# A four-layer image network: the mixers' statistics taken from their Fourier modes, and where the third layer's tiles lie

## The chip, the cores and the metric

One Trainium2 chip, one of its cores, one kernel launch. The time is the device time of one execution in microseconds (us), the median of three runs. The engines are PE (matrix products and transposes, results in PSUM), ACT (one activation function per pass, with a scale and a bias per partition), DVE (vector work, reductions and normalisation statistics), POOL (slower vector work), and SP, which here only starts transfers. A transfer can be started from SP's queue or from ACT's; the start itself then stands in that engine's queue. All data is 32-bit float.

## The reference

Four images of 64 x 64 positions with 128 channels go through four residual layers, `x = x + layer_n(_gn(x))`, where `_gn` is a group normalisation over groups of four channels: a selective-scan layer, a Fourier layer with a feed-forward part, an attention between channels in Fourier space ("CoDANO"), and a neighbourhood attention. The change is in the third one. There every channel is a token, a 64 x 64 picture, and every `instance_norm` is over a picture. What matters is its end, after the attention:

```python
def instance_norm(x, g, b):
    mu = jnp.mean(x, axis=(-2, -1), keepdims=True)
    var = jnp.var(x, axis=(-2, -1), keepdims=True)
    return (x - mu) * jax.lax.rsqrt(var + EPS) * g[:, None, None] + b[:, None, None]

def spectral_conv(x, w, out_shape):
    wc = w[..., 0] + 1j * w[..., 1]          # 32 x 17 modes
    ...
    xft = jnp.fft.rfftn(x, axes=(-2, -1), norm='forward')
    top = jnp.einsum('bihw,iohw->bohw', xft[:, :, :mh, :mw], wc[:, :, :mh])
    bot = jnp.einsum('bihw,iohw->bohw', xft[:, :, -mh:, :mw], wc[:, :, mh:])
    ...
    return jnp.fft.irfftn(out_ft, s=out_shape, axes=(-2, -1), norm='forward')

def fno_layer(x, spec_w, skip_w, skip_b, out_shape, norm=None, act=None):
    xs = fourier_resample(conv1x1(x, skip_w, skip_b), out_shape)
    xf = spectral_conv(x, spec_w, out_shape)
    if norm is not None:
        xf = instance_norm(xf, *norm)
    y = xf + xs
    return act(y) if act is not None else y

# inside codano_forward, at its end
attn = instance_norm(attn + tokens, attn_norm_g, attn_norm_b)
m = instance_norm(attn, norm2_g, norm2_b)
m = fno_layer(m, mixer_w1, mixer_skip_w1, mixer_skip_b1, (H, W), norm=(mixer_norm_g1, mixer_norm_b1), act=_gelu)
m = fno_layer(m, mixer_w2, mixer_skip_w2, mixer_skip_b2, (H, W), norm=(mixer_norm_g2, mixer_norm_b2))
out = instance_norm(m, mixer_out_g, mixer_out_b) + attn
```

The mean and the variance of `xf` are functions of its few modes: by Parseval, the mean is the mode (0, 0), and the variance is a weighted sum of the squares of the others.

## The kernel before

The code counts its layers from 0 and this text from one: the first layer is `layer0`, the second `layer1`, the third `layer2`, the fourth `layer3`. In the profile the first layer takes the span up to 5752 us, the second 5752 to 6230, the third 6230 to 7211, the fourth the rest.

**Memory and waits.** Tiles come from pools, laid one after another in a partition's bytes. A pool opened where a closed pool lay must wait for the old users of those bytes. With `reuse_waits="tile"` each tile waits only for the users of the earlier tiles under it; otherwise all tiles of the new pool wait for all users of the pools it falls on. The second layer's pools wait by tile; the third's (`layer2`, L1713) and the fourth's (L1735) by pool. In the second layer the pool `l1big` comes first, then `l1tmp`.

**Second layer** (`layer1`, L962). For each image `layer1_spectrum` makes `hT` (two buffers in `l1tmp`) from the image `x1`, the weights `w1` and `w2` and, for its second axis, a transposed copy `xa` of the image. `layer1_feed` then goes through eight chunks c of 512 positions: four products into `pf`, four Relu on ACT (L914) into `h1`, sixteen products into `po` (L926), a layer norm on DVE, the addition to x (L945), and a store on SP's queue (L946). The feed of one image runs beside the spectrum of the next; the last image's feed has nothing beside it. SP's queue is in the order written; the other engines are put in order by a scheduler. `layer2_weights` (L1005) loads and prepares the third layer's constants meanwhile.

**Third layer** (`layer2`, L1713). `layer2_image` (L1202) is a generator that yields between steps, and two images run in turn. `Pace` (L1112) holds a model of each engine's costs; its `in_turn` always advances the image whose modelled time is earliest, and that fixes the order in which PE, ACT, DVE and POOL run their work. A `yield True` says that the next step needs the last one's result; `nc.aside` marks work that does not move the image's modelled time. All its instructions are recorded at one line, L1155, so groups are told apart by tile names.

The mixers begin after the attention's `z` has its statistics. `spectral` (L1607) takes a picture tile (`z`, later `m`; 128 positions x 32 x 128 channels):

- `dft_y`: eight groups of four products into `pu`, each copied by ACT into `U`.
- four `pq` (two products of 512 columns each), each multiplied by the mode weights on DVE into `Zp` (68 rows: real and imaginary parts in four forms times 17 frequencies; 64 channel pairs x 32).
- `synthesis`: four steps, each two `pa` (copied by ACT into `S`, tile tag S2) and two `pb`, one for u = 0 and one for u = 1; a `pb` holds four position blocks of 128 channels and goes to the function `put`. For `spectral` that is `copied`: ACT copies it into `sp`, DVE counts it with four bn_stats, and a piece of side work is given to POOL.

`token_stats` turns the counts into mean and variance with eight small products `in_pm` and two DVE operations between them; `norm_scale` takes the square root on ACT and the reciprocal on DVE.

Mixer 1 scales `sp` with q1 and f1 and adds it to `m` (= z times A2) chunk by chunk (four chunks of 1024): even chunks by eight ACT activations (`affine`), odd ones by two whole-chunk DVE operations (`by_rows`), then an addition on DVE and the gelu on ACT. Its side work is `residual` (L1642): it loads the layer's input `xr` and makes `z*sa + za + xr` on POOL. Mixer 2's side work is `grown`, `m * scal(10)` on POOL. Mixer 2 adds `sp*q2` to `m` by 32 scalar_tensor_tensor (stt) on DVE, counts `m` with 32 bn_stats, and the end makes `m*q3 + f3 + z`: three chunks by ACT and a DVE addition, the last by eight stt and one `by_rows` on DVE; each chunk is stored from SP.

The fourth layer's constants and edges are loaded at its start (L1760 and following).

Of the kernel before, what the change touches and what calls it, by code (L numbers as in the profile page):

```python
# [11 lines left out]
F32 = mybir.dt.float32  # L12
# [5 lines left out]
P = 128  # L18
# [782 lines left out]
def layer1_weights(sh, A, wp, wq):  # L801
# [4 lines left out]
    for name, pool in (("w1", wp), ("w2", wq)):  # L806
        w[name] = pool.tile([P, 16, 2, P], F32, name=name)
        nc.sync.dma_start(w[name], A[name])
# [8 lines left out]
    w["sy"] = wq.tile([P, 256], F32, name="c_sy1")  # L817
# [4 lines left out]
def layer1_spectrum(sh, w, pools, x_dram, x, norm, out):  # L822
# [17 lines left out]
    hT = out["hT"] = tmp.tile([P, NT], F32, name="hT", bufs=2)  # L840
    for axis in range(2):
# [18 lines left out]
        if axis == 0:  # L860
            out["xa"] = big.tile([P, NJ, DM], F32, name="xa", bufs=1)
            xv = x_dram.rearrange("(h w2 w1) d -> w1 h w2 d", w1=2, w2=32)
            for q in range(2):
                nc.sync.dma_start(out["xa"][64 * q : 64 * q + 64], xv[q])
# [40 lines left out]
def layer1_feed(sh, w, pools, x, hT, x_out):  # L905
# [12 lines left out]
    for c in range(NCH):  # L918
# [27 lines left out]
        nc.sync.dma_start(x_out[c * CH : (c + 1) * CH, :].rearrange("(j p) d -> p j d", p=P), xc)  # L946
# [14 lines left out]
def layer1(sh, A, x_in, x_out, l2w, wt, ahead):  # L961

    tc, nc = sh.tc, sh.nc
    with ExitStack() as ctx:
# [4 lines left out]
        pools |= {"small": pool("l1small", 2), "ps": pool("l1ps", 4, space=PSUM)}  # L969
        w = layer1_weights(sh, A, pools["tmp"], pools["big"])  # L970
# [3 lines left out]
        with tc.manual_schedule(engines=engines):  # L974
            for b in range(NB + 1):
                out = {}
# [13 lines left out]
                if b < NB:  # L990
                    fed = layer1_feed(sh, w, pools, x, out["hT"], x_out(b))
# [13 lines left out]
def layer2_weights(sh, A, wp, setup, ps, wt, w):  # L1005
# [18 lines left out]
    for n in (1, 2):  # L1024
        load(f"mix{n}", [Q, 32], A[f"mix{n}"])
    pa, pb, vra, vrb, via, vib = (load(name, [Q, 32, 16], A[name], setup) for name in ("pa", "pb", "vra", "vrb", "via", "vib"))
# [22 lines left out]
    for n in (1, 2):  # L1049
        m = w[f"mix{n}"]  # L1050
        nc.vector.tensor_scalar(m, m, qc[:, 0:1], None, ALU.mult)
# [138 lines left out]
def layer2_image(sh, w, pools, x_in, x_out, scr, wt, parity, beside):  # L1190
# [75 lines left out]
    def dft_y(src, scale=None, then=None):  # L1266

        U = large("U2", [P, 2, 32, 64])
        for g in range(NJ // 4):
# [7 lines left out]
            else:  # L1277
                nc.scalar.activation(Ug, pg, AF.Copy, scale=scale)
                then(g)
# [327 lines left out]
    def spectral(src, mix, beside=()):  # L1607
        beside = iter(beside)
        U = yield from dft_y(src)
        Zm = own([Q, 64, 32], "Zp", tmp)  # L1610
        for g in range(4):
            px = ps.tile([Q, 32, 16], F32, name="pq", tag="b")
            for q in range(2):
                nc.tensor.matmul(
                    px, lhsT=w["quad"][:, q, :], rhs=U[:, q, :, 16 * g : 16 * g + 16], start=(q == 0), stop=(q == 1)
                )
            tt(
                Zm[:, 16 * g : 16 * g + 16, :],
                px.rearrange("p r t -> p t r"),
                mix.unsqueeze(1).to_broadcast([Q, 16, 32]),  # L1620
                ALU.mult,
            )
            yield g == 3
        sp = large("sp")
        st = own([P, NJ, 6], "in_st")

        def copied(u, g0, p):
            nc.scalar.copy(at(sp, u, g0), p)
            counted(st, sp, block(u, g0))
            nc.aside = True  # L1630
            next(beside, None)
            nc.aside = False

        yield from synthesis(Zm, copied)
        return sp, st


    m = large("m")
    for c in range(4):
        by_rows(m, z, A2, c, ALU.mult)  # L1640
    yield False
    def residual():  # L1642
        xr = large("xr")
        load_image(nc, xr, x_in)
        for n, c in enumerate(C4):
# [3 lines left out]
            if n % 2:  # L1649
                yield  # L1650

    sp, st = yield from spectral(z, w["mix1"], residual())
    mu, var = yield from token_stats(sp, st)
# [44 lines left out]
    yield True  # L1698
    for n, c in enumerate(C4):
        rows = slice(1024 * n, 1024 * n + 1024)  # L1700
        if n == 3:
# [7 lines left out]
        nc.sync.dma_start(x_out[rows, :].rearrange("(j p) d -> p j d", p=P), m[:, c, :])  # L1709
# [292 lines left out]
def constants():  # L2002
# [48 lines left out]
    qc[:, :, 6] = np.array([0, 1, 0, 1])[:, None]  # L2051
    c["c_qcol"] = qc.reshape(Q, 8)

# [14 lines left out]
def lay_out(i):  # L2068
# [52 lines left out]
    for n in (1, 2):  # L2121
        m = L2[f"mixer_w{n}"][0, 0].transpose(1, 0, 2)
        a[f"mix{n}"] = quad([m[..., 0], m[..., 1], m[..., 0], m[..., 1]])
    p = L2["proj_w"][:, 0].transpose(2, 1, 0, 3)
# [58 lines left out]
```

## Time and profile before

The profiled execution took 7781.59 us, of which the span is 7779.7; the three runs took 7775.43 to 7779.66 with a median of 7777.08. A table of the last three layers, from the windows of the trace and its start times:

| stretch | from | to | us |
|---|---|---|---|
| second layer | 5752 | 6230 | 478 |
| third layer, first pair: to its mixers' stretch | 6230 | 6475 | 245 |
| third layer, first pair: that stretch | 6475 | 6723 | 248 |
| third layer, second pair: to its mixers' stretch | 6723 | 6961 | 238 |
| third layer, second pair: that stretch | 6961 | 7211 | 250 |
| fourth layer | 7211 | 7780 | 569 |

A row of the window view gives the length of the window, each engine's busy time with the number of instructions, the clock that PE was granted as a share of full speed, and the transfer engines' load. A row of the timeline gives start, length, engine, line, operation, `out<-in` by the program's names, shapes, the number of instructions run together, and in brackets how long the engine had stood idle and what ended that. The chain of waits goes back from the last instruction to what released it; its rows are start, length and what it was. Where two durations overlap in a row, the records are those of a pipeline and the next start tells the pitch.

### The profile page before, as it was taken

The numbers are of one execution on the slowest core, as the hardware profiler recorded it, in microseconds if no ns is written. First come the engines' busy times: TensorE is split into PE (matmuls) and PEld (weight loads), VectorE is DVE, ScalarE is ACT, GpSimd is POOL, SyncE is SP. The second block draws the span as 40 slices with busy tenths as digits, with TensorE's granted clock in tenths as the row PEclk, the third lists the DMA queues.
The fourth block names the chain that finished last, engine by engine and source line by source line (L and its number), as shares of the span: only waits on it lengthen the run. The fifth ranks groups of instructions, "written<-read, shape, count | busy, mean of one in ns | idle before, by whom it ended". The sixth has DMA issues, their size and how long they took to land. (4 is left out here: it accounts for less than half of the span.)

```text
span 7779.7 us, 141035 instructions
## 1 busy us (share of the span) xinstructions
PE 6337.0 (81%) x52796; PEld 3998.2 (51%) x52796; DVE 6747.1 (87%) x8097; ACT 6112.9 (79%) x9715; POOL 5675.9 (73%) x2590
## 2 busy tenths in 40 slices
PE   7888888878889877888887777787779968687789
PEld 3544444444455444445554444444457756564566
DVE  7999999999999999999999999999966646556678
ACT  7999999989999998999999999999843323314667
POOL 4989999988999998999999999999930023223233
PEclk8999999999999999999999999999999978788899
DMA  6555556545565554555655445455532142231332
GB/s 171 173 163 175 174 173 176 170 169 165 186 183 179 185 177 162 163 177 179 180 184 180 168 156 185 160 188 177 181 107 63 43 128 61 71 108 40 103 95 81
DMA packets 1325855, 1158.87 MB, mean 149 GB/s; under 512 B 694133, under 2 KB 1119697, under 8 KB 1258226
## 3 DMA queue, kind: packets, MB, share of 16 engines
q1 hardware_dynamic: 1323010, 1148.47, 48.0%
q8 instruction: 416, 6.82, 0.4%
q14 instruction: 269, 2.20, 0.1%
q10 hardware_dynamic: 2160, 1.38, 0.1%
HBM read 956.37 MB, written 189.21 MB: 147 GB/s over the span
## 5 line engine op out<-in xcount | busy, mean ns | idle before, releaser
L688 DVE TENSOR_TENSOR_SCAN h<-dA,state,dB 128x512 f32<-128x512 f32 x4096 | 4921.0, 1266 | 204.4 <-POOL dB L682 79.5
L682 POOL TENSOR_TENSOR dB<-du,Bb 128x1024 f32<-128x1024 f32 x2048 | 4811.7, 2385 | 342.9 <-DVE h L688 208.6
L538 PE MATMUL pt<-ident,h 128*128 128x128 f32 x16384 | 2221.0, 279 | 875.7 <-ACT hT L548 860.0
L687 ACT ACTIVATE dA<-delta,A_neg 128x512 f32<-128x512 f32 x4096 | 2761.1, 697 | 157.6 <-DVE h L688 129.7
L538 PEld LDWEIGHTS pt<-ident,h 128*128 128x128 f32 x16384 | 1807.0, 142 | 1926.3 <-ACT hT L548 1704.7
L548 ACT COPY hT<-pt 128x1024 f32<-128x1024 f32 x2048 | 2080.2, 1016 | 164.7 <-PE pt L538 146.4
L573 PE MATMUL yT<-hT,W 128*32 128x256 f32 x16384 | 1379.6, 409 | 0.4
L573 PEld LDWEIGHTS yT<-hT,W 128*32 128x32 f32 x16384 | 456.0, 150 | 342.5 <-issue 330.9
L161 PE MATMUL cv<-xn,taps 128*128 128x512 f32 x936 | 527.0, 644 | 2.8 <-DVE delta L474 2.8
L1155 POOL TENSOR_TENSOR xg<-xg,so 128x1024 f32<-128x1024 f32 x16 | 39.3, 2466 | 636.5 <-PE pu L1155 613.6
L1900 POOL TENSOR_TENSOR S<-S,sm 128x784 f32<-128x784 f32 x128 | 191.1, 1493 | 419.1 <-DVE sm L1898 256.3
L477 POOL TENSOR_TENSOR du<-delta,u 128x1024 f32<-128x1024 f32 x128 | 304.3, 2377 | 79.0 <-DVE delta L474 78.9
L465 PE MATMUL dp<-xd,w_dt 65*128 65x512 f32 x512 | 288.8, 646 | 69.9 <-ACT Ct L456 47.0
L448 PE MATMUL xd_ps<-u,w_x 128*48 128x512 f32 x512 | 251.8, 615 | 23.6 <-DVE e L360 18.1
L1907 ACT ACTIVATE S<-S,mx 128x196 f32<-128x196 f32 x512 | 227.8, 448 | 35.9 <-DVE mx L1934 35.4
L161 PEld LDWEIGHTS cv<-xn,taps 128*128 128x128 f32 x936 | 139.2, 188 | 180.5 <-issue 160.4
L914 ACT ACTIVATE h<-pf,b 128x512 f32<-128x512 f32 x128 | 87.7, 687 | 117.2 <-PE pf L913 99.2
L474 DVE SCALAR_TENSOR_TENSOR delta<-delta,dp 128x512 f32<-128x512 f32 x256 | 170.6, 667 | 4.3 <-ACT delta L471 1.0
L1862 PE MATMUL pt<-ident,S 128*98 128x128 f32 x1024 | 166.3, 287 | 3.5 <-POOL S L1900 2.0
L465 PEld LDWEIGHTS dp<-xd,w_dt 65*128 65x128 f32 x512 | 76.5, 188 | 174.5 <-ACT Ct L456 99.9
L1155 POOL TENSOR_TENSOR WX<-wr,Xs 128x544 f32<-128x544 f32 x40 | 58.0, 1449 | 148.2 <-issue 61.8
L471 ACT ACTIVATE delta<-delta 128x512 f32<-128x512 f32 x256 | 165.9, 649 | 0.0
(378 smaller groups left out, 7030.6 us busy)
## 6 DMA issues: line engine op xcount, KB each, us to landing
Bb<-l_B SPq DMA_DIRECT2D x512, 1024.0 KB
W<-l_W SPq DMA_DIRECT2D x512, 256.0 KB
l_y<-y SPq DMA_DIRECT2D x127, 512.0 KB
u<-l_xr SPq DMA_DIRECT2D x64, 512.0 KB
u<-l_xw SPq DMA_DIRECT2D x64, 512.0 KB
y<-l_y SPq DMA_DIRECT2D x56, 512.0 KB
V<-l_v SPq DMA_DIRECT2D x512, 49.0 KB
y<-l_y SPq DMA_DIRECT2D x80, 256.0 KB
```

The lines of the kernel that those rows point to most:

```text
L161: nc.tensor.matmul(pm, lhsT=taps[:, s, t, :], rhs=xn[:, dy : dy + 8, dx : dx + 64], start=(t == 0), stop=(t == 8),)
L448: nc.tensor.matmul(bank["x"], lhsT=w_x[:, s, k, :], rhs=u[:, s, :], start=(s == 0), stop=(s == 1))
L465: nc.tensor.matmul(bank[s], lhsT=w_dt[:, k, s * P : (s + 1) * P], rhs=xd, start=True, stop=True)
L477: nc.gpsimd.tensor_tensor(du, delta, u, ALU.mult)
L538: nc.tensor.transpose(pt[:, j, s, :], G["h"][:, s, t0 : t0 + 32, :].rearrange("p t n -> p (t n)"), sh.ident)
L548: return lambda: nc.scalar.copy(hT, pt.rearrange("p j s d -> p j (s d)"))
L573: nc.tensor.matmul(U["yT"][e][32 * jo : 32 * jo + 32, qo % 2, :], lhsT=U["Ws"][G["g"]][:, :, 4 * q + j], rhs=hT[:, j, :], start=((e, jo) n ...
L682: nc.gpsimd.tensor_tensor(dB, du, B_now[:, q : q + 1, :].to_broadcast([P, 2, CH]), ALU.mult)
L687: nc.scalar.activation(dA, delta[:, s, :], AF.Exp, scale=A_neg[:, k, s, n : n + 1])
L688: nc.vector.tensor_tensor_scan(h[:, s, :, q], dA, dB[:, s, :], state[:, s, n : n + 1], ALU.mult, ALU.add)
L1900: nc.gpsimd.tensor_tensor(Sv, Sv, U["sm"].unsqueeze(2).to_broadcast([P, 4, 196]), ALU.mult)
L1907: nc.scalar.activation(Sn, Sn, AF.Exp, bias=U["mx"][:, n : n + 1], accum_out=sm[:, n : n + 1])
```

## The change

In the second layer `w2`, `xa` and the constant `sy` move from `l1big` to `l1tmp`. `hT`, two buffers in `l1tmp` before, is one tile at the head of `l1tmp` (images 0 and 2) and one in `l1big` (images 1 and 3). In bytes of a partition, the tiles that the last image's feed uses (two x1, two h1, two h2, hT, ff0, ff1, b0, rows) are then the first 73.5 KB; the third layer's pools `l2tmp` and `l2small`, some 80 KB, lie over them, and `xg`, the first tile of its pool `l2big`, behind. The last image's feed stores its chunks 4 to 7 from ACT's queue. The third layer's pools wait by tile. In the mixers `spectral` gets the statistics from the modes in `Zp` before the synthesis: products `pn` with a table `power`, squares on ACT, sums on DVE, products `pm`. The synthesis then puts its results from PSUM straight into `m`, and `sp` is gone. `residual` and `grown` are given to POOL at other places, and the first chunk of the end goes to POOL. Two new weights (`mir1`, `mir2`) and a table `once` bring the modes of frequency 0 into a form in which each is counted once.

```diff
@@ -803,7 +803,7 @@
     nc.sync.dma_start(w["an"], A["c_an1"])
-    for name, pool in (("w1", wp), ("w2", wq)):
+    for name, pool in (("w1", wp), ("w2", wp)):
         w[name] = pool.tile([P, 16, 2, P], F32, name=name)
@@ -814,7 +814,7 @@
     nc.scalar.dma_start(w["rows"], A["l1_rows"].partition_broadcast(P))
-    w["sy"] = wq.tile([P, 256], F32, name="c_sy1")
+    w["sy"] = wp.tile([P, 256], F32, name="c_sy1")
     nc.scalar.dma_start(w["sy"], A["c_sy1"])
@@ -837,7 +837,9 @@
-    hT = out["hT"] = tmp.tile([P, NT], F32, name="hT", bufs=2)
+    if out["hT"] is None:
+        out["hT"] = (big if out["b"] % 2 else tmp).tile([P, NT], F32, name="hT")
+    hT = out["hT"]
     for axis in range(2):
@@ -858,7 +860,7 @@
         if axis == 0:
-            out["xa"] = big.tile([P, NJ, DM], F32, name="xa", bufs=1)
+            out["xa"] = tmp.tile([P, NJ, DM], F32, name="xa")
             xv = x_dram.rearrange("(h w2 w1) d -> w1 h w2 d", w1=2, w2=32)
@@ -902,7 +904,7 @@
-def layer1_feed(sh, w, pools, x, hT, x_out):
+def layer1_feed(sh, w, pools, x, hT, x_out, last):
@@ -943,7 +945,8 @@
         nc.vector.tensor_tensor(xc, xc, h2, ALU.add)
-        nc.sync.dma_start(x_out[c * CH : (c + 1) * CH, :].rearrange("(j p) d -> p j d", p=P), xc)
+        eng = nc.scalar if last and c >= 4 else nc.sync
+        eng.dma_start(x_out[c * CH : (c + 1) * CH, :].rearrange("(j p) d -> p j d", p=P), xc)
         yield
@@ -967,13 +970,14 @@
         pools |= {"small": pool("l1small", 2), "ps": pool("l1ps", 4, space=PSUM)}
+        hT = pools["tmp"].tile([P, NT], F32, name="hT")
         w = layer1_weights(sh, A, pools["tmp"], pools["big"])
 ...
             for b in range(NB + 1):
-                out = {}
+                out = dict(b=b, hT=hT if b == 0 else None)
                 if b < NB:
@@ -988,7 +992,7 @@
                 if b < NB:
-                    fed = layer1_feed(sh, w, pools, x, out["hT"], x_out(b))
+                    fed = layer1_feed(sh, w, pools, x, out["hT"], x_out(b), b == NB - 1)
                 if b == 1:
@@ -1023,6 +1027,9 @@
         load(f"mix{n}", [Q, 32], A[f"mix{n}"])
+        load(f"mir{n}", [Q, 32], A[f"mir{n}"], setup)
+    load("power", [Q, 226], A["c_power"])
+    once = load("once", [Q, 32], A["c_once"], setup)
     pa, pb, vra, vrb, via, vib = (load(name, [Q, 32, 16], A[name], setup) for name in ("pa", "pb", "vra", "vrb", "via", "vib"))
@@ -1048,7 +1055,8 @@
         m = w[f"mix{n}"]
-        nc.vector.tensor_scalar(m, m, qc[:, 0:1], None, ALU.mult)
+        nc.vector.scalar_tensor_tensor(m, m, qc[:, 0:1], once, ALU.mult, ALU.mult)
+        nc.vector.scalar_tensor_tensor(m, w[f"mir{n}"], qc[:, 7:8], m, ALU.mult, ALU.add)
@@ -1276,6 +1284,7 @@
                 nc.scalar.activation(Ug, pg, AF.Copy, scale=scale)
+            if then is not None:
                 then(g)
@@ -1604,41 +1613,39 @@
-    def spectral(src, mix, beside=()):
-        beside = iter(beside)
-        U = yield from dft_y(src)
+    def spectral(src, mix, then=None):
+        U = yield from dft_y(src, None, then)
         Zm = own([Q, 64, 32], "Zp", tmp)
+        total = own([P, NJ, 6], "in_st")[0:34].rearrange("p j k -> p (j k)")[:, 0:128].rearrange("p (n t) -> p n t", n=2)
         for g in range(4):
+            part = slice(16 * g, 16 * g + 16)
             px = ps.tile([Q, 32, 16], F32, name="pq", tag="b")
             for q in range(2):
+                nc.tensor.matmul(px, lhsT=w["quad"][:, q, :], rhs=U[:, q, :, part], start=(q == 0), stop=(q == 1))
+            tt(Zm[:, part, :], px.rearrange("p r t -> p t r"), mix.unsqueeze(1).to_broadcast([Q, 16, 32]), ALU.mult)
+            yield False
+            pn = ps.tile([34, 16, 32], F32, name="pn", tag="a")
+            nc.tensor.matmul(pn, lhsT=w["power"][:, 0:34], rhs=Zm[:, part, :], start=True, stop=True)
+            sq = tmp.tile([34, 16, 32], F32, name="sq", tag="S2", bufs=3)
+            nc.scalar.activation(sq, pn, AF.Square)
+            nc.vector.tensor_reduce(total[:, 0, part], sq[:, :, 1:32], AX.X, ALU.add)
+            nc.vector.tensor_copy(total[:, 1, part], sq[:, :, 0])
+            yield g == 3
+        pm = held([P, 2, NJ], "in_pm")
+        for u in range(2):
+            half = slice(64 * u, 64 * u + 64)
+            nc.tensor.matmul(pm[half, 0, :], lhsT=w["power"][:, 162:226], rhs=Zm[:, u:64:2, 0], start=True, stop=True)
+            for n in range(2):
                 nc.tensor.matmul(
-                    px, lhsT=w["quad"][:, q, :], rhs=U[:, q, :, 16 * g : 16 * g + 16], start=(q == 0), stop=(q == 1)
+                    pm[half, 1, :],
+                    lhsT=w["power"][0:34, 34 + 64 * n : 98 + 64 * n],
+                    rhs=total[:, n, u:64:2],
+                    start=(n == 0),
+                    stop=(n == 1),
                 )
-            tt(
-                Zm[:, 16 * g : 16 * g + 16, :],
-                px.rearrange("p r t -> p t r"),
-                mix.unsqueeze(1).to_broadcast([Q, 16, 32]),
-                ALU.mult,
-            )
-            yield g == 3
-        sp = large("sp")
-        st = own([P, NJ, 6], "in_st")
-
-        def copied(u, g0, p):
-            nc.scalar.copy(at(sp, u, g0), p)
-            counted(st, sp, block(u, g0))
-            nc.aside = True
-            next(beside, None)
-            nc.aside = False
-
-        yield from synthesis(Zm, copied)
-        return sp, st
-
-
-    m = large("m")
-    for c in range(4):
-        by_rows(m, z, A2, c, ALU.mult)
-    yield False
+        yield True
+        return Zm, pm[:, 0, :], pm[:, 1, :]
+
     def residual():
@@ -1646,11 +1653,20 @@
                 nc.gpsimd.tensor_tensor(z[:, c, :], z[:, c, :], v, op)
-            if n % 2:
-                yield
-
-    sp, st = yield from spectral(z, w["mix1"], residual())
-    mu, var = yield from token_stats(sp, st)
+            yield
+
+    rest = residual()
+
+    def aside(works):
+        nc.aside = True
+        next(works, None)
+        nc.aside = False
+
+    m = large("m")
+    for c in range(4):
+        by_rows(m, z, A2, c, ALU.mult)
+    yield False
+    Zm, mu, var = yield from spectral(z, w["mix1"])
     vs = col("vs")
@@ -1660,45 +1676,71 @@
     yield True
-    for c in range(5):
-        if c < 4:
-            if c % 2:
-                by_rows(m, m, f1, c, ALU.add)
-                by_rows(sp, sp, q1, c, ALU.mult)
-            else:
-                affine(sp, sp, q1, f1, c)
-            mc = m[:, C4[c], :]
-            tt(mc, mc, sp[:, C4[c], :], ALU.add)
-        if c > 0:
-            mc = m[:, C4[c - 1], :]
+    for c in range(4):
+        if c in (0, 1, 2, 3):
+            by_rows(m, m, f1, c, ALU.add)
+        else:
+            for j in range(8 * c, 8 * c + 8):
+                nc.scalar.activation(m[:, j, :], m[:, j, :], AF.Identity, bias=f1[:, j : j + 1])
+        yield False
+
+    def mixed(u, g0, p):
+        for n, j in enumerate(block(u, g0)):
+            stt(m[:, j, :], p[:, n, :], q1[:, j : j + 1], m[:, j, :], ALU.mult, ALU.add)
+        if u == 1:
+            mc = m[:, C4[g0 // 4], :]
             nc.scalar.activation(mc, mc, AF.Gelu)
-        yield c == 4
-
-
-    def grown():
-        for n, c in enumerate(C4):
-            nc.gpsimd.tensor_scalar(m[:, c, :], m[:, c, :], scal(10), None, ALU.mult)
-            yield
-
-    sp, st = yield from spectral(m, w["mix2"], grown())
-    mu, var = yield from token_stats(sp, st)
+            if (0, 0, 0, 0)[g0 // 4] == 0:
+                aside(rest)
+
+    yield from synthesis(Zm, mixed)
+
+    def grown(g):
+        if g % 2:
+            nc.aside = True
+            mc = m[:, C4[g // 2], :]
+            nc.gpsimd.tensor_scalar(mc, mc, scal(10), None, ALU.mult)
+            nc.aside = False
+
+    Zm, mu, var = yield from spectral(m, w["mix2"], grown)
     q2 = yield from norm_scale(var, 12, "q2")
 ...
     st = own([P, NJ, 6], "in_st")
-    for n in range(4):
-        js = range(8 * n, 8 * n + 8)
-        for j in js:
-            stt(m[:, j, :], sp[:, j, :], q2[:, j : j + 1], m[:, j, :], ALU.mult, ALU.add)
-        counted(st, m, js)
-        yield n == 3
+
+    def summed(u, g0, p):
+        if u in (1,):
+            t = tmp.tile([P, 4, DM], F32, name="qs", tag="S2", bufs=3)
+            for n, j in enumerate(block(u, g0)):
+                nc.scalar.activation(t[:, n, :], p[:, n, :], AF.Copy, scale=q2[:, j : j + 1])
+            tt(at(m, u, g0), at(m, u, g0), t, ALU.add)
+        for n, j in enumerate(block(u, g0) if u not in (1,) else ()):
+            stt(m[:, j, :], p[:, n, :], q2[:, j : j + 1], m[:, j, :], ALU.mult, ALU.add)
+        counted(st, m, block(u, g0))
+        if u == 1 and (0, 0, 0, 0)[g0 // 4] == 1:
+            aside(rest)
+
+    yield from synthesis(Zm, summed)
     mu, var = yield from token_stats(m, st)
 ...
     yield True
+    def put(n):
+        rows = slice(1024 * n, 1024 * n + 1024)
+        nc.sync.dma_start(x_out[rows, :].rearrange("(j p) d -> p j d", p=P), m[:, C4[n], :])
+
+    wide = lambda v, c: v[:, c].unsqueeze(2).to_broadcast([P, 8, DM])
+    for n in (0,):
+        c = C4[n]
+        nc.aside = True
+        for v, op in ((wide(q3, c), ALU.mult), (wide(f3, c), ALU.add), (z[:, c, :], ALU.add)):
+            nc.gpsimd.tensor_tensor(m[:, c, :], m[:, c, :], v, op)
+        nc.aside = False
+        put(n)
     for n, c in enumerate(C4):
-        rows = slice(1024 * n, 1024 * n + 1024)
-        if n == 3:
+        if n in (0,):
+            continue
+        if n in (3,):
             for j in range(8 * n, 8 * n + 8):
@@ -1706,14 +1748,16 @@
             tt(m[:, c, :], m[:, c, :], z[:, c, :], ALU.add)
-        nc.sync.dma_start(x_out[rows, :].rearrange("(j p) d -> p j d", p=P), m[:, c, :])
+        put(n)
         yield n == 3
 ...
     with ExitStack() as ctx:
-        pool = lambda name, bufs, **kw: ctx.enter_context(tc.tile_pool(name=name, bufs=bufs, **kw))
+        pool = lambda name, bufs, **kw: ctx.enter_context(
+            tc.tile_pool(name=name, bufs=bufs, reuse_waits="tile", **kw)
+        )
         ps = pool("l2ps", 3, space=PSUM)
@@ -2049,7 +2093,20 @@
     qc[:, :, 6] = np.array([0, 1, 0, 1])[:, None]
+    qc[:, :, 7] = np.array([1, 1, 1, -1])[:, None]
     c["c_qcol"] = qc.reshape(Q, 8)
...
```

The tile `hT` of `l1tmp` is one buffer: image 2 draws it there again under the same name. `power` holds the weights of the sums (square root of 2 per mode, of a half at frequency 0), columns of ones, and the columns that pick the mode (0, 0).

More of the change, by code (lines that the diff above doesn't have):

```diff
@@ L2051, in constants @@
     qc[:, :, 6] = np.array([0, 1, 0, 1])[:, None]
+    qc[:, :, 7] = np.array([1, 1, 1, -1])[:, None]
     c["c_qcol"] = qc.reshape(Q, 8)
+    power = np.zeros((4, 17, 226))
+    for k in range(17):
+        power[0:2, k, k] = power[2:4, k, 17 + k] = 2.0**0.5 if k else 0.5**0.5
+    power[0:2, 0, 162:226] = 1.0
+    power = power.reshape(Q, 226)
+    power[0:34, 34:162] = 1.0
+    power[[0, 17], 98:162] = 0.0
+    c["c_power"] = power
+    once = np.ones((4, 17, 32))
+    once[:, 0, 17:] = 0.0
+    c["c_once"] = once.reshape(Q, 32)
     sc = np.zeros((128, 3, 6))
@@ L2123, in lay_out @@
         a[f"mix{n}"] = quad([m[..., 0], m[..., 1], m[..., 0], m[..., 1]])
+        m = np.concatenate([np.zeros_like(m[:1, :1]), m[:1, :16:-1], np.zeros_like(m[:1, :16])], 1)
+        a[f"mir{n}"] = quad([m[..., 0], m[..., 1], m[..., 0], m[..., 1]])
     p = L2["proj_w"][:, 0].transpose(2, 1, 0, 3)
```

## The prediction

> **What bounds the kernel now.** First the table of windows at the layer boundaries, since the shares of the whole span describe the first layer (5752 of 7779.7 us), which the diff does not touch.
>
> ```profile
> core 0: us, PE busy (x) PEld busy (x) DVE busy (x) ACT busy (x) POOL busy (x), PEclk, DMA share, GB/s
> 5752.00:6230.00 478.00, 437.17 (x2797) 356.27 (x2796) 284.92 (x759) 150.66 (x260) 0.00 (x0) 0.97 0.25 60
> ...
> 6475.00:6723.00 248.00, 179.31 (x812) 119.12 (x812) 156.72 (x469) 109.58 (x213) 74.61 (x32) 0.82 0.19 49
> ...
> 6961.00:7211.00 250.00, 174.85 (x800) 114.70 (x800) 156.66 (x470) 109.87 (x214) 76.44 (x40) 0.82 0.15 40
> ```
>
> The two 248 to 250 us rows are the third layer's last stretch, once for each pair of images. No engine is busy for three quarters of it and the granted clock falls to 0.82: it is bound by waits. The mixers themselves run from the first `pu` (6514.4 and 7000.2) to the last `m` on DVE (6722.5 and 7207.6), 207.4 us in the second pair. The timeline of PE shows where it stood:
>
> ```profile
> 7060.40 2.04 PE L1155 MATMUL pb<-S,bd 64*128 64x512 f32 x8
> 7064.74 0.64 PE L1155 MATMUL in_pm<-in_st,tok 128*128 128x32 f32 x4 [2.30 <-DVE in_st L1155]
> ...
> 7078.17 3.78 PE L1155 MATMUL pu<-an,m 128*128 128x128 f32 x16 [8.57 <-ACT m L1155]
> ...
> 7095.64 6.94 PE L1155 MATMUL pu<-an,m 128*128 128x128 f32 x40 [11.81 <-ACT U L1155]
> ...
> 7162.52 1.06 PE L1155 MATMUL in_pm<-in_st,tok 128*128 128x32 f32 x4 [6.03 <-DVE in_st L1155]
> ...
> 7187.34 1.04 PE L1155 MATMUL in_pm<-in_st,tok 128*128 128x32 f32 x4 [19.50 <-DVE in_st L1155]
> ```
>
> PE runs without a gap while spectra are made (7000.0 to 7062.4, 7095.6 to 7156.5) and stands while `sp` is counted, scaled and added: 2.3+2.7+8.6+0.2+11.8 us after mixer 1, 6.0+19.5+1.8 after mixer 2, then to the end. The chain of waits has that end:
>
> ```profile
> 7187.19 2.10 DVE m L1155 x8
> ...
> 7193.65 9.35 ACT m L1155 x24
> 7203.02 3.33 DVE m L1155 x9
> 7206.37 1.24 DVE m L1155
> 7207.62 3.19 DMA x<-m
> ```
>
> And at 6227.56 the third layer waits for the second's last store before it loads:
>
> ```profile
> 6226.84 0.70 DVE x L945
> 6227.56 2.27 DMA x<-x
> 6230.03 4.19 DMA xg<-x
> ...
> 6241.94 0.38 DVE gn_mv L1155
> ```
>
> **Part 1, the boundary (tiles moved, stores c>=4 on ACT, waits by tile).** `xg` no longer lies on bytes that the last feed uses, so its loads may be issued once SP is through with store c=3 (its `x` ends at 6201.5). Loads took 4.2 us, so `xg` is there some 10 us before DVE ends its last `x` (6227.5). Then 8 bn_stats follow it by 0.65 each (three took 1.96): `gn_mv` at 6232.8 instead of 6241.9, a gain of 9. Bounds 0 (the loads are still held) and 10. Four triggers on ACT are about 0.4 us each (the first layer's ACT triggers, L427); the one for c=4 waits for `x` at 6208.5, and behind it stand the next chunk's four Relu, which before were due at 6210.2: 1.7 us of slack cover it. The last store (7 of 8) no longer blocks anything but its own landing. At the layer's start `w2` and `xa` lie in another pool; `xa` was asked for at 5755.7 and needed at 5778.7, 23 us of cover, so 0, with up to 3 lost.
>
> **Part 2, set-up in the second layer.** Four small loads and two DVE operations of 128x32 size (0.2 each): DVE is busy for 285 of that window's 478 us. 0.
>
> **Part 3, PE's work in the mixers.** Per image and mixer before: dft 8 groups at 0.89, 4 `pq` at 1.72, 8 `pa` and `pb` pairs, 3.85 per step of four, 15.4 in all: 29.4, and 1.6 for the three groups of `in_pm`. After: the same 29.4, 4 `pn` of 512 columns (half of a two-matmul `pq`, 0.86 each, 3.4), 6 small `pm` at 0.26 (1.5): 34.3. Four such per pair are 137.2. The trace's own gapless stretch lasted 62.4 where these rows give 60.5 (two times 29.4 and 1.8 of `in_pm`), 3% more: **141 us**. PE's cost thus rises by some 13 us a pair; what pays is the idle time.
>
> **Part 4, statistics before synthesis.** Gone per call: 8 ACT copies of `sp` (0.53 to 0.59), 32 bn_stats (4 x 1.65 = 6.6 of DVE), the two-step token statistics. New: 4 Square on ACT (0.59 as a 128x512 copy), 4 reductions on DVE (34x496; the nearest row, 128x512, took 0.69) and 4 small copies (0.16): 3.4 on DVE, each hidden under the next `pq`, which is 1.72 of PE. The last one is not: Square 0.6, reduce 0.7, copy 0.2, `pm` 1.5, then a chain of small operations before q1 and f1 are there. In the trace the chain from `vs` (7064.6) to `f` (7072.3) took 7.7 us, since every other small operation was held behind POOL:
>
> ```profile
> 7034.68 0.67 DVE L1155 TENSOR_TENSOR Zp<-pq,mix 68x512 f32<-68x512 f32 x1
> ...
> 7066.23 0.23 DVE L1155 TENSOR_TENSOR in_d<-in_st,in_pm 128x64 f32<-128x64 f32 x1
> 7066.50 1.98 DVE L1155 TENSOR_TENSOR in_d<-in_d 128x64 f32<-128x64 f32 x1
> ```
>
> The same operation is 0.23 with one operand in PSUM and 1.98 with two in SBUF, ending with a POOL `z` operation (7066.05 to 7068.39); `Zp`, read from PSUM, is not slowed. Now POOL's residual starts only after the statistics of its own image, so the chain costs 3 (free) to 9 us (under the other image's POOL). The Trainium skill, "SBUF — State Buffer", Who interferes with whom, speaks against this change: a VectorE instruction with two SBUF inputs, or a copy in its two-port mode, and a GpSimd instruction that reads SBUF lock each other out for a whole instruction. It agrees with the 1.98 and 0.23; by it alone the new copies and every `m += f1` would be held and the sum would be rival A's; by the rows, with POOL's work after the statistics, it is the one below.
>
> **Part 5, putting.** Mixer 1: 4 `m += f1` per image on DVE (1.14 pitch alone; the row m<-z,A averaged 1.64, up to 2.9 beside POOL), then 4 stt of 0.27 per put from PSUM (the SBUF form took 2.2 per 8) and a gelu per chunk (1.05): 8 puts x 1.1 = 8.8 of DVE under 15.4 of PE. Gone are the 16 affine (6.4 of ACT), 2 `sp*q1` and 4 adds after the spectrum. While one image waits for its statistics or its `m += f1`, PE has the other's dft and `pq`. Mixer 2: half the puts by stt, half by 4 ACT copies (1.6) and one add (0.6 to 0.7), plus 32 bn_stats (6.6): DVE 4.4+2.8+6.6 = 13.8 under 15.4 of PE. That removes 32 stt and 32 bn_stats (15 us an image) from behind the spectrum, where 7162.5 to 7187.3 lay.
>
> **Gaps.** PE's idle time inside the mixers was 53 a pair. What is left I price at **12**: one chain of 9 in mixer 1 that the other image does not cover, 3 in mixer 2 (gelu and U copies before the first `pu`). Bounds 4 (only the last chain) and 36 (9 for each of the four image-mixers).
>
> **End.** From the last synthesis matmul: last put and bn_stats 3, token statistics, q3, f3 6.4 (7187.2 to 7193.6), then the tail. Before: ACT 9.35, DVE 3.33+1.24 = 14. After: POOL takes chunk 0 (1.9+1.9+2.35 = 6.2), ACT two chunks (6.2), tt 1.2, DVE chunk 3 about 3.4 of stt and add: 11 to 12.5. **21** in all; bounds 18 and 27 (chunk 3's add held behind POOL, and a slow start of q3).
>
> **Sum.** 141+12+21 = 174 against 207.4: 33.4 a pair, 66.8 for two; extremes 137+4+18 = 159 (gain 48) and 141+36+27 = 204 (gain 3). Third to fourth layer: the fourth's set-up loads wait for the last user of the S2 buffers (SP waited 103 us at L1760, loads at 7156.6, first needs at 7226.9); that user now ends some 20 us before the end rather than 51. The set-up took 13 us, so it still fits: 0, at worst 5 lost. Total 67+9 = 76: the profiled execution's 7781.6 (span 7779.7 and 1.9 around it) becomes 7705.6; it lies 4.5 above the runs' median of 7777.1, so the median is **7701**.
>
> **Rivals.** *Better than that*: the gaps nearly vanish, 4+18, both images overlap throughout: two times 48 and 9 off 7777, 7672. For it: DVE has 76 us of slack a pair. Against it: every image-mixer keeps one statistics chain that PE must wait for.
>
> *A, DVE under POOL's lock is the bound.* POOL works 76 us of the window; `m += f1` at 2.9, copies and small operations at 1.3 to 2.0. Gaps 30, end 25: 196, gain 11.4 a pair, 7777-23-9 = 7745. For it: the 1.98 row. Against it: the new wide operations read PSUM.
>
> *B, the mixers give nothing* (extra PE work equals the removed idle), only the boundary: 7768.
>
> *C, slower.* PE's queue is in written order: when the first `pa`/`pb` of one image stands at its head waiting for `m += f1` (the put holds the PSUM buffer), the other image's work behind it waits too. If each of the four image-mixers exposes its chain of 12.5 and mixer 1 also four adds of 2.9, that is 73; 141+73+23 = 237, 30 a pair lost, 7777+59-9 = 7827. It decides from 11.4 us exposed per image-mixer ((207.4-141-21)/4). For it: the order comes from a model of costs that knows no POOL lock. Against it: before, mixer 1's spectra of both images ran on PE 62 us without a gap.
>
> **How the numbers follow.** Main case 0.69 (7680 to 7730 by gaps 5 to 28), better 0.06, A 0.13, B 0.04, C 0.08. The time is the main case's 7701; the range 7670 to 7746 takes in the better case's centre and A's. A measurement of this kernel tells about 0.2% (15.5 us) from no change: faster is main, better and A, 0.88; same is B, 0.04; slower is C, 0.08.
>
> **What would show it.** `xg` loads issued near 6202 and `gn_mv` near 6233; `pn` at 0.86; no bn_stats on `sp`; PE's longest wait inside the mixers under 12 us and its granted clock there above 0.82; the mixers 170 to 180 us from first `pu` to last `m`; POOL's three operations in the tail ending before chunk 3. I am wrong if `xg` is still loaded after the last store, if `m += f1` takes 2.9 on PE's path in both images, or if the squares hold `pq` back by more than a buffer.

## The result: 0.2% slower

The changed kernel took 7793.5 us, the kernel before 7777.7 (medians of 17 runs each), a ratio of 1.0020 with a 95% interval of 1.0013 to 1.0027. The profiled execution took 7795.28 us with a span of 7793.5. Its windows, with the columns of the table of before:

```profile
5752.00:6230.00 478.00, 440.35 (x2819) 359.23 (x2818) 289.00 (x763) 150.49 (x260) 0.00 (x0) 0.98 0.30 69
...
6475.00:6723.00 248.00, 200.50 (x806) 115.12 (x806) 166.88 (x391) 86.97 (x174) 94.03 (x38) 0.83 0.15 41
...
6961.00:7211.00 250.00, 212.36 (x843) 122.62 (x841) 159.60 (x376) 90.88 (x181) 95.84 (x46) 0.83 0.09 23
```

PE is busy 37.5 us longer in the last window than before, ACT 19 us less, and the clock is hardly higher (0.83, before 0.82). The boundary went as forecast (SP, then DVE, in order of time):

```profile
6199.62 24.10 SPq L1163 DMA_DIRECT2D xg<-x  x8
```

```profile
6224.52 0.69 DVE L947 TENSOR_TENSOR x<-x,h 128x512 f32<-128x512 f32 x1
...
6231.17 0.37 DVE L1163 BATCH_NORM_AGGREGATE gn_mv<-gn_st 128x2 f32<-128x48 f32 x1
```

From the end of the second layer's last `x` to `gn_mv` it is 6.0 us; before it was 14.4. The mixers lost more than that: 217 and 219 us for the two pairs, from the first `pu` of z to the last `m`, where they took 208 before. PE's timeline in the second pair:

```profile
7001.54 14.28 PE L1163 MATMUL pu<-an,z 128*128 128x128 f32 x104
...
7028.58 1.89 PE L1163 MATMUL pn<-Zp,power 68*34 68x512 f32 x2 [10.15 <-DVE Zp L1163]
...
7059.80 0.42 PE L1163 MATMUL in_pm<-in_st,power 34*64 34x32 f32 x2 [2.83 <-DVE in_st L1163]
...
7062.32 7.19 PE L1163 MATMUL pa<-sy,Zp 68*128 68x256 f32 x16
7069.44 3.79 PE L1163 MATMUL pb<-S,bd 64*128 64x512 f32 x8
...
7102.11 1.99 PE L1163 MATMUL pa<-sy,Zp 68*128 68x256 f32 x8
```

Two things are new. PE stands 10 us ahead of the first `pn`, behind which all its other work waits. And from 7062 on the eight records of a row of `pa` or `pb` take 3.7 us instead of 1.9, without a gap on record. Windows of 2 us name the reason, the granted clock (third number from the end):

```profile
7084.00:7086.00 2.00, 2.00 (x5) 1.64 (x6) 1.08 (x4) 0.88 (x1) 0.00 (x0) 0.50 0.00 0
...
7096.00:7098.00 2.00, 2.00 (x11) 1.16 (x11) 0.95 (x4) 1.02 (x2) 0.00 (x0) 1.00 0.00 0
```

The clock is at half for 37 us, from 7058 to 7095, and from 7061 on the record shows PE busy all the time; DVE stood idle for 9.7 us of it. One row in it hides a wait: the eight `pb` from 7076.88 on took 7.0 us, and at the same place of the first pair the profile has

```profile
6584.10 3.75 PE L1163 MATMUL pb<-S,bd 64*128 64x512 f32 x4 [3.34 <-DVE m L1163]
```

There the clock had come back (eight `pa` from 6576.86 on in 1.99 us) and was at half again behind that wait. Why `Zp` came late, the timelines of DVE and POOL show:

```profile
7007.57 20.26 DVE L1163 TENSOR_TENSOR m<-z,A 128x1024 f32<-128x1024 f32 x8
7027.76 0.68 DVE L1163 TENSOR_TENSOR Zp<-pq,mix 68x512 f32<-68x512 f32 x1
```

```profile
7008.93 2.75 POOL L1163 TENSOR_TENSOR z<-z,sa 128x1024 f32<-128x1024 f32 x1 [49.49 <-DVE m L1163]
7011.75 2.76 POOL L1163 TENSOR_TENSOR z<-z,za 128x1024 f32<-128x1024 f32 x1
7014.59 3.21 POOL L1163 TENSOR_TENSOR z<-z,xr 128x1024 f32<-128x1024 f32 x1
```

POOL's residual starts as soon as the first `m<-z,A` has read z, not where it stands in the program, and both engines slow down: the eight `m<-z,A` take 20.3 us, before 12.6, and POOL's `z<-z,sa` 2.75 us, where it takes 1.90 alone. Before, POOL stood after two operations, because `xr` was not there yet. The kernel before, DVE and then POOL:

```profile
7006.05 12.57 DVE L1155 TENSOR_TENSOR m<-z,A 128x1024 f32<-128x1024 f32 x8
```

```profile
7010.24 2.75 POOL L1155 TENSOR_TENSOR z<-z,za 128x1024 f32<-128x1024 f32 x1
7027.99 2.35 POOL L1155 TENSOR_TENSOR z<-z,xr 128x1024 f32<-128x1024 f32 x1 [15.00 <-DMA xr<-x]
```

An account for four kernels, second pair, from the first `pu` of z to the last `m`. Idle is PE's; "clock" sums, over windows of 1 us, PE's busy time times one minus the granted clock; the end runs from the last `pb`; the work is what remains, waits hidden inside a row included.

| us | work | idle | clock | end | sum |
|---|---|---|---|---|---|
| forecast | 141 | 12 | 0 | 21 | 174 |
| before | 122.7 | 26.1 | 7.6 | 51.1 | 207.5 |
| changed | 144.1 | 17.6 | 27.7 | 29.2 | 218.6 |
| hold (below) | 143.7 | 4.2 | 10.0 | 29.2 | 187.1 |
| warm128 (below) | 150.0 | 13.6 | 12.6 | 29.2 | 205.4 |

### The profile page after: what moved, and what is told of

It is laid out like the page before. It is cut to its first block, busy times and chain, and to the rows that moved or that the text cites. A ratio compares the mean times of both kernels' runs of the same rounds, so it can differ in the third digit from the quotient of the medians.

```text
span 7793.5 us, 141003 instructions
## 1 busy us (share of the span) xinstructions
PE 6406.7 (82%) x52860; PEld 4013.4 (51%) x52860; DVE 6771.5 (87%) x7951; ACT 6074.7 (78%) x9651; POOL 5716.6 (73%) x2602
```

## Experiments

Ratios are to the kernel before, in runs on the same chip.

**POOL's residual held back.** DVE copies sa after the four `m += f1` of an image, and POOL reads the copy.

```diff
-            for v, op in ((wide(sa), ALU.mult), (wide(za), ALU.add), (xr[:, c, :], ALU.add)):
+            for v, op in ((wide(held_sa[0]), ALU.mult), (wide(za), ALU.add), (xr[:, c, :], ALU.add)):
...
+    sa2 = vs
+    nc.nc.vector.tensor_scalar(sa2, sa, 1.0, None, ALU.mult)
+    held_sa.append(sa2)
```

> The changed kernel (7793.5 us), but POOL's residual reads a copy of sa that DVE makes only after the four m+=f1 of the same image, so POOL cannot start while DVE still makes m<-z,A. Theory (POOL's lock on DVE starts the loss): the eight m<-z,A take 9 to 11 us instead of 20.2, PE's wait of 10.2 us before the first pn falls below 2, q1 and f1 come without operations of 1.7 to 2.0 us, and each pair gains 10 to 25 us, the upper half if the clock also stays up: 7745 to 7774. Rival (the written order of PE's queue makes the loss, whoever DVE shares with): the wait moves by a few us and the time stays within 7 us of 7793.

Measured: 7738.1 us, 0.9949 (0.9932 to 0.9965). Its DVE and PE in the first pair:

```profile
6507.06 9.16 DVE L1163 TENSOR_TENSOR m<-z,A 128x1024 f32<-128x1024 f32 x8
```

```profile
6518.10 1.02 PE L1163 MATMUL pn<-Zp,power 68*34 68x512 f32 x2
...
6545.24 7.19 PE L1163 MATMUL pa<-sy,Zp 68*128 68x256 f32 x16
...
6568.45 1.99 PE L1163 MATMUL pb<-S,bd 64*128 64x512 f32 x8
```

```profile
6546.00:6564.00 18.00, 18.00 (x41) 9.96 (x40) 13.75 (x25) 6.06 (x9) 12.33 (x5) 0.50 0.01 1
```

The wait ahead of `pn` is gone, `m<-z,A` is at 1.15 each, and the time falls by 0.7% against the changed kernel, more than forecast: in the second pair less idle time (4 instead of 18 us) and less lost to the clock (10 instead of 28). The rival falls: PE's order was the same. The clock is still at half from 6544 to 6564, without a gap on record, though PE had not stood longer than 1.3 us before.

**The residual left out.**

```diff
-        for n, c in enumerate(C4):
-            wide = lambda v: v[:, c].unsqueeze(2).to_broadcast([P, 8, DM])
-            for v, op in ((wide(sa), ALU.mult), (wide(za), ALU.add), (xr[:, c, :], ALU.add)):
-                nc.gpsimd.tensor_tensor(z[:, c, :], z[:, c, :], v, op)
-            yield
+        nc.gpsimd.tensor_tensor(z[:, 0:1, 0:8], z[:, 0:1, 0:8], xr[:, 0:1, 0:8], ALU.add)
+        yield
```

> The changed kernel without POOL's residual: z stays the attention's sum, only 8 columns of xr are added, so the output lacks the scaling of z and the layer's input. Theory (POOL's lock on DVE's operations with two SBUF inputs makes the loss): m<-z,A 9 to 10 us for eight, m<-m,f 1.2 each, PE idle in mixer 1 under 4 us a pair, and the time of the run with the residual held or up to 12 below it: 7726 to 7740. If holding the residual helped by something else than the lock, this run stays above 7760.

Measured: 7741.6 us, 0.9948 (0.9932 to 0.9965), mixers of 191.1 and 186.5 us against 191.1 and 187.1 in the run with the residual held. So holding it recovers all that it cost, as far as these runs can tell. In the first and the second pair 14 and 10 us are still lost to the clock without any residual.

**The buffer of xr.** `sp` took one of seven large buffers. Without it SP loaded `xr` of the second pair at 6955.68, before at 7023.74. This run takes the buffer again:

```diff
         pm = held([P, 2, NJ], "in_pm")
+        if then is None:
+            nc.nc.vector.memset(large("sp")[:, 0, 0:8], 0.0)
```

> The changed kernel with one thing given back: in mixer 1 each image again takes a large buffer named sp after its spectrum (DVE writes 8 columns of it, nothing reads it), so xr gets its buffer as late as it did before. Theory (the buffer that sp no longer needs let xr be loaded some 70 us earlier, so POOL's residual ran against DVE's m<-z,A): xr is loaded after the first spectrum again, the eight m<-z,A take 12 to 15 us instead of 20.3, PE's wait before the first pn falls from 10 us to 5 or less, and the time falls by 8 to 25: 7768 to 7785. Rival (m<-z,A is slow for another reason, as the new work on ACT and PE): no change, 7790 to 7797.

Measured: 7791.6 us, 1.0018 (1.0008 to 1.0027). SP, DVE and PE in the first pair:

```profile
6545.36 11.03 SPq L1163 DMA_DIRECT2D xr<-x  x8
```

```profile
6512.76 12.57 DVE L1163 TENSOR_TENSOR m<-z,A 128x1024 f32<-128x1024 f32 x8
```

```profile
6526.07 1.02 PE L1163 MATMUL pn<-Zp,power 68*34 68x512 f32 x2 [2.74 <-DVE Zp L1163]
...
6556.30 0.42 PE L1163 MATMUL in_pm<-in_st,power 34*64 34x32 f32 x2 [5.71 <-DVE in_st L1163]
...
6582.53 3.75 PE L1163 MATMUL pb<-S,bd 64*128 64x512 f32 x4 [8.86 <-DVE m L1163]
```

The mechanism is as expected (12.57 again, a wait of 2.7), but the time is not: the later residual meets the statistics and `m += f1` instead, and PE waits 5.7 and 8.9 us there. So the early `xr` only chose the place. The cost comes with the new DVE operations that PE waits for, wherever POOL meets them.

**The clock.** Four products into a PSUM tile that nothing reads, ahead of mixer 1's synthesis, with 128 rows and with 64.

```diff
+    pd = ps.tile([P, CH], F32, name="pd", tag="a")
+    for n in range(4):
+        nc.nc.tensor.matmul(pd, lhsT=w["an"], rhs=Us[0][0:128, 0, 8 * n : 8 * n + 8, :].rearrange("p r t -> p (r t)"), start=True, stop=True)
     yield from synthesis(Zm, mixed)
```

> The changed kernel with four extra products of 128 rows and 512 columns per image, into a PSUM tile that nothing reads, just ahead of mixer 1's synthesis. Theory (PE is at half clock through the synthesis, where pa and pb have 68 and 64 rows, and comes back late): the extra work of 128 rows lifts the clock within 7 us, pa and pb go at 1.9 us per eight instead of 3.7, and after paying 4 x 0.9 to 1.7 per image each pair gains 5 to 15 us: 7763 to 7784. Rival (pa and pb are slow because they wait for DVE and ACT to free PSUM): the extra work only adds, 7800 to 7821.

> The same four extra products per image at the same place with 64 rows. If the clock only asks that PE is busy, this does what the run with 128 rows does, within 5 us. If it asks for rows in use, the clock stays at 0.5 in the synthesis of mixer 1 and the time is 7 to 28 us above the changed kernel: 7800 to 7821.

Measured: with 128 rows 7767.4 us, 0.9986 (0.9976 to 0.9995); with 64 rows 7780.3 us, 1.0001 (0.9992 to 1.0011). PE in the second pair, 128 rows and then 64:

```profile
7043.92 5.40 PE L1700 MATMUL pd<-U,an 128*128 128x512 f32 x8
7049.16 3.62 PE L1163 MATMUL pa<-sy,Zp 68*128 68x256 f32 x16
```

```profile
7048.98 6.74 PE L1700 MATMUL pd<-U,bd 64*128 64x512 f32 x8
7055.65 7.20 PE L1163 MATMUL pa<-sy,Zp 68*128 68x256 f32 x16
7062.78 3.79 PE L1163 MATMUL pb<-S,bd 64*128 64x512 f32 x8
7066.50 1.99 PE L1163 MATMUL pa<-sy,Zp 68*128 68x256 f32 x8
```

More work made the kernel faster, which excludes the rival as the whole cause, though one row of `pb` did wait in the changed kernel. After 128-row products `pa` goes at full clock at once; after 64-row ones only 17.5 us after their start. The run with 64 rows missed its expectation of 7800 to 7821: even so its clock came back earlier than in the changed kernel (13 us of busy time lost in mixer 1 instead of 23), and PE's idle time there was 13 instead of 16 to 20 us. Against the changed kernel it gained 0.2% (1.0020 to 1.0001), the run with 128 rows 0.3%: about half of the gain does not need 128 rows. Why the idle time fell, in both runs, was not followed further.

**The clock with the residual held, and the tail.** Three runs on top of the run with the residual held: DVE's chunk 3 first in the tail (hold3); the same with three 128-row products per image in PE's last waits of mixer 1's spectrum (hold3w); and the tail of before (holdtail).

```diff
-    for n, c in enumerate(C4):          # hold3; holdtail drops POOL's chunk instead
-        if n in (0,):
-            continue
+    for n in (3, 1, 2):
+        c = C4[n]
...
+        warm(2)                         # hold3w, ahead of pm; warm(1) ahead of the last pn
```

> The run with POOL's residual held (7738 us), and in the tail DVE's own chunk 3 goes ahead of the chunks 1 and 2 that it must wait for ACT to scale. Theory (the tail of 29 us after the last pb is made of DVE's written order and of POOL's lock): DVE no longer stands 3.3 us for ACT, 2 to 4 us are gained in the second pair and up to 4 in the first: 7731 to 7737. Rival (the tail is bound by ACT's 6.3 us and the stores): nothing, 7736 to 7740.

> The run before this one with three extra products of 128 rows per image in the places where PE waits at the end of mixer 1's spectrum (one before the last pn, two before pm). Theory (half clock through the synthesis costs what is left, 22 us of half clock in each pair): pa and pb go at full clock from the start or within 4 us, each pair gains 5 to 11 less 2 to 4 of extra work: 7718 to 7733. Rival (with the residual held PE's clock no longer bounds the mixers): 0 to 8 slower than the run before.

> The run with POOL's residual held, with the tail of the kernel before: chunks 0, 1 and 2 on ACT, nothing on POOL. If POOL's three operations pay as forecast (chunk 0 off ACT's path), this is 2 to 4 us slower for each pair, 7740 to 7748. If their lock costs DVE as much as they save (in_d 1.9, q and f 1.75, m<-m,z 2.2 instead of 0.2 and 1.2), it is the same or up to 6 faster: 7732 to 7740.

Measured: 7742.4 us, 0.9958 (0.9943 to 0.9972); 7751.5 us, 0.9966 (0.9953 to 0.9979); 7741.3 us, 0.9954 (0.9937 to 0.9970). None can be told from the run with the residual held, and the theories of hold3 and hold3w missed. The end stays at 28 to 29 us in all of them: neither POOL's share nor DVE's order makes its length. In hold3w the clock still fell to half around 6556, with PE's waits filled and PE busy on record throughout:

```profile
6546.00:6554.00 8.00, 8.00 (x29) 3.16 (x28) 5.62 (x14) 1.50 (x3) 0.00 (x0) 1.00 0.99 257
6556.00:6562.00 6.00, 6.00 (x14) 2.61 (x13) 5.89 (x9) 2.53 (x4) 2.57 (x1) 0.50 0.00 0
```

The extra products cost what they brought.

**One mixer at a time.** `m2only` has mixer 1 of before and mixer 2 as changed, `m1only` the reverse; boundary and tail as changed.

```diff
-    Zm, mu, var = yield from spectral(z, w["mix1"])                  # m2only
+    sp, st = yield from spectral_old(z, w["mix1"], rest)
+    mu, var = yield from token_stats(sp, st)
...
-    Zm, mu, var = yield from spectral(m, w["mix2"], grown)           # m1only
+    sp, st = yield from spectral_old(m, w["mix2"], grown())
+    mu, var = yield from token_stats(sp, st)
```

> The changed kernel with mixer 1 as it was before (sp, its counts, the scaling and adding after the spectrum, POOL's residual beside the synthesis); boundary, mixer 2 and tail as changed. Theory (mixer 1's part makes the whole loss, by POOL's lock and by PE's half clock; mixer 2's part and the boundary gain): from the first pu of z to the first of m some 78 us as before instead of 104 to 108, mixer 2 as in the changed kernel (about 85 to the last pb and 29 behind it), so 95 + 29 + ... = 192 a pair, 7793 - 2 x 25 = 7735 to 7755. Rival (both mixers lose in the changed form): 7770 to 7793.

> The reverse: mixer 1 and the tail as changed, mixer 2 as before (sp, its counts, 32 stt and 32 bn_stats behind the spectrum). Theory: mixer 1 keeps its 104 to 108 us from pu of z to pu of m and mixer 2 goes back to 78 us and some 45 to 51 behind the last pb, so each pair is 10 to 20 us longer than in the changed kernel: 7810 to 7835. Rival (mixer 2's part gives nothing): 7785 to 7800.

Measured: 7764.7 us, 0.9982 (0.9972 to 0.9991), and 7837.0 us, 1.0072 (1.0057 to 1.0087). With mixer 1 as before, the stretch to the first `pu` of m is 78 us again; as changed it is 104 to 111. So mixer 1's part loses about 0.4% (1.0020 against 0.9982), and mixer 2's part gains 0.5% (against 1.0072). With the residual held that stretch is 78 to 80 us in the changed form too, so mixer 1's part then loses nothing there. `m2only` is 10 us over its range: its images no longer run side by side in mixer 2 (PE begins the statistics of m 33 us apart, at 7144.7 and 7178.1; in the changed kernel 15.5), and from the first `pu` of m to the last `pb` it is 101 us where it was 80 to 85.

**The boundary alone.** The kernel before with the tiles moved, the four stores on ACT and the third layer's pools waiting by tile.

> The kernel before with the boundary's part alone: w2, xa, sy and hT moved, the last image's stores c>=4 on ACT's queue, the third layer's pools waiting by tile; the mixers are those of before. Both theories: gn_mv 9 us earlier as in the changed kernel, and all of it kept: 7766 to 7771. If the mixers' loss came from the tile moves (later or earlier buffers), this run would lose too.

Measured: 7777.0 us, 0.9995 (0.9986 to 1.0005): unclear, and above its 7766 to 7771. In its profile `gn_mv` follows the last `x` by 6.0 us as in the changed kernel, so the 8.4 us are there, and the first `pu` of z comes 7.6 us earlier than before in the first pair and 6.7 us earlier in the second. Over the whole run the interval reaches from 11 us gained to 4 lost and cannot show whether they are kept to the end.

**Two thirds of the residual on ACT.** `z*sa+za` by ACT behind each gelu of mixer 1, only `+xr` on POOL.

```diff
-            for v, op in ((wide(sa), ALU.mult), (wide(za), ALU.add), (xr[:, c, :], ALU.add)):
-                nc.gpsimd.tensor_tensor(z[:, c, :], z[:, c, :], v, op)
+            affine(z, z, sa, za, n)
+            nc.gpsimd.tensor_tensor(z[:, c, :], z[:, c, :], xr[:, c, :], ALU.add)
```

> The changed kernel with two thirds of the residual moved from POOL to ACT: z*sa+za by 32 activations per image behind each gelu of mixer 1 (so it cannot start early), and only the addition of xr on POOL (2.35 us per chunk). Theory: DVE is hardly locked, m<-z,A takes 9 to 10 us; ACT takes 3.2 us more per chunk between copies of S that PE waits for. If ACT has the room (it was busy 87 of 248 us), 7725 to 7745; if the copies of S come late in the synthesis, 7745 to 7770.

Measured: 7775.2 us, 0.9995 (0.9985 to 1.0004): 5 us above the worse of its two expectations. `m<-z,A` takes 9.2 us, but PE now waits for copies of S behind those activations:

```profile
6572.52 2.08 PE L1163 MATMUL pa<-sy,Zp 68*128 68x256 f32 x4 [2.29 <-ACT S L1163]
...
6594.20 3.78 PE L1163 MATMUL pa<-sy,Zp 68*128 68x256 f32 x8 [3.54 <-ACT S L1163]
```

From the first `pu` of m to the last `pb` it is 98 us, with the residual held 80 to 82.

## Why the prediction was wrong

It forecast 7701 with 0.08 for slower.

- **PE's work, 141 us a pair, was nearly right**: 144.1. It rose by 21 us, where Part 3 had some 13. `pn`, `pm` and the boundary's `gn_mv` were right too.
- **The failed steps are the clock in Part 3 and the overlap in Part 4.** The second pair took 218.6 us instead of 174: of the 44.6 us more, the clock makes 27.7, the end 8.2, the gaps 5.6 and the work 3.1.
- **The clock (Part 3).** The 141 us were taken at the clock of a gapless stretch, whose first 5 us (7000 to 7005) ran at half clock and so cover the 3% added; no other term stood for the clock, though the prediction itself read 0.82 in the first view. Measured, it was 22.7 and 27.7 us a pair. In the kernel before, half clock fell mostly into PE's waits, where it is free (7.6 us lost); in the changed one it falls into the synthesis. The runs with extra products show the clock as a cause.
- **The overlap (Part 4): "POOL's residual starts only after the statistics of its own image" was false**, and rival A, dismissed for it, held the mechanism, though not its size (7745) nor the operation that paid, `m<-z,A`. The timeline of before had POOL's first `z` operation right behind `m<-z,A` and then a wait of 15 us for `xr`: its start was set by data, not by its place. Holding it gives 0.7%, some 55 of the 92 us between forecast and measurement; part of that comes by way of the clock (10 to 15 us a pair are left of 23 to 28).
- **Gaps**: 12 forecast; 17.6 and 21.4 measured, 10 to 11 of it ahead of the first `pn`. Of rival C the structure was right (PE's written order passes one image's wait to both), its place was not: it was `Zp` behind `m<-z,A`, not `m += f1` (in the run that takes the buffer of `xr` again it was the statistics and `m += f1`). Two of the signs named ahead could not tell: PE's longest wait, 11.0 us, was under 12, and the granted clock, 0.83, above 0.82.
- **Luck**: with the residual held the time, 7738, lies in the range of the forecast, but not by its sum: 4 us of gaps instead of 12, 10 to 15 lost to the clock instead of none, an end of 29 instead of 21.
- **End**: 21 forecast, 29 measured. Both images now end together, so that two tails share ACT and DVE. DVE after the last scaling by ACT, for both images:

```profile
7208.94 3.36 DVE L1163 TENSOR_TENSOR m<-m,z 128x1024 f32<-128x1024 f32 x2 [3.31 <-ACT m L1163]
7212.22 2.18 DVE L1163 SCALAR_TENSOR_TENSOR m<-m,q,z 128x128 f32<-128x128 f32 x8
7214.43 1.23 DVE L1163 TENSOR_TENSOR m<-m,f 128x1024 f32<-128x1024 f32 x1
7215.58 1.22 DVE L1163 TENSOR_TENSOR m<-m,z 128x1024 f32<-128x1024 f32 x1
7216.71 2.19 DVE L1163 SCALAR_TENSOR_TENSOR m<-m,q,z 128x128 f32<-128x128 f32 x8
7218.93 1.22 DVE L1163 TENSOR_TENSOR m<-m,f 128x1024 f32<-128x1024 f32 x1
```

`m2only` tells what that is worth, since its second image comes 33 us behind and its tail runs alone. Its last `pb` and last `m`, second pair (PE and DVE):

```profile
7166.15 5.25 PE L1163 MATMUL pb<-S,bd 64*128 64x512 f32 x16
```

```profile
7194.37 1.23 DVE L1163 TENSOR_TENSOR m<-m,f 128x1024 f32<-128x1024 f32 x1
```

Between their ends lie 24.2 us, so the second tail makes some 5 of the 8 us at most; in the first pair, where DVE also begins the next pair's work, it is 27.9. What makes the rest was not tested; in that end of 24.2 us the last count of `m` comes 6.6 us after the last `pb`, where the forecast had 3.

The Trainium skill's rule that spoke against the change ("SBUF — State Buffer", Who interferes with whom) was the one to follow: `m<-z,A` has two SBUF inputs and took 2.5 us beside POOL and 1.15 alone (20.26 and 9.16 for eight).

## What to carry to other kernels

Ask of every side job not where it stands in the program but which data lets it start, and which operations it meets then; a copy of one small operand, made at the right moment, holds it (0.7% here). When work moves out of PE's waits onto PE, price it at the clock that those waits leave behind: here half of full speed for 20 us and more.

## What the hardware showed unexpectedly

With products of 64 and 68 rows PE stayed at half clock for long: 20 us without a gap on record in the run with the residual held, 17.5 us from the first 64-row product on in warm64, and 37 us in the changed kernel, where a hidden wait may have prolonged it. Four products of 128 rows brought the clock back within their 5.4 us (it was at half for some 3.5 us in the second pair of warm128). The Trainium skill ("TensorE: Matmul & The Clock Gate", Part 1: The HAM clock gate) has the full clock after one busy window of some 3.4 us; these runs agree for 128 rows and not for 64. The clock also fell while PE had no wait above 1.3 us, and in hold3w while it had none on record. Few rows alone do not hold it down: in mixer 2 of the changed kernel `pa` and `pb` ran at full clock from 7164 to 7178 with nothing between them. Whether the clock follows the rows in use or another measure of the array's activity, the runs do not settle.
